# Layer 1 of a two-layer attention kernel: the head mixing as sixteen 32x32 products, transposed back on VectorE

## The chip, the cores and the metric

The kernel runs on one core of a Trainium2 chip. The metric is the device time of one execution, in microseconds, and everything is float32. The core's engines are named as in the profile: PE (TensorE, the matmuls), PEld (its weight loads), DVE (VectorE), ACT (ScalarE), POOL (GpSimd), SP (SyncE, which issues most of the DMAs). PE writes to PSUM only; DVE and ACT carry results from there to SBUF.

## The reference: what is computed

Eight images of 512 channels and 1024 tokens pass through two attention layers, each with a residual. The change is in the second one; a group norm stands before it:

```python
q, k, v = (einsum('oc,bct->bot', w, xf).reshape(b, heads, hd, t) for w in (w_q, w_k, w_v))
attn = einsum('bhdq,bhdT->bhqT', q, k) * scale
attn = einsum('gh,bhqT->bgqT', w_head, attn)          # heads are mixed before the softmax
attn = softmax(attn, axis=-1)
mean, var = attn.mean((-2, -1)), attn.var((-2, -1))   # one pair for each image and head
attn = (attn - mean) / sqrt(var + eps) * in_gamma + in_beta
out = einsum('bhqT,bhdT->bhqd', attn, v)
out = out.reshape(b, t, c) @ w_proj.T + b_proj        # without swapping heads and queries first
```

There are 8 heads of 64 channels. Since the heads are mixed before the softmax, all eight scores of a query and a key must meet before the exponential is taken. The variance over an image's whole attention map needs the sum of e and of e squared of each query and head, where e is the exponential.

## The kernel before, in words

Layer 0 takes all eight images first; layer 1 then takes them one after the other. The order of the instructions on PE, ACT, DVE, POOL and SP is the order in which the code issues them (`manual_schedule`); nothing reorders them later.

**One image in layer 1** is 32 steps x. Each handles 256 queries, 256 keys and half of the heads for the scores, and, four or five steps later, half of the keys of such a block for the rest (`half_step`, which issues everything; the lag is `MLAG`). A step has these parts:

- `scores` (L1656, twice a step): 64x64 products, four of them side by side in the array, give scores with queries on partitions. ACT (L1671) or, for some, DVE (L1669) copies them to the tile `raw`.
- `regroup` (L1680): a DMA takes every eighth partition of `raw`, so 16 queries with their 8 heads, and lays them out in the tile `re` as 128 partitions of (query, head). Each is held behind one particular matmul, so that they go one at a time.
- `mix` (L1704): `re` is the stationary operand, 64 rows of (8 queries, 8 heads) by 64 keys; the moving one is `wmix`, a block matrix of the head weights, 64 columns wide. Four 64x64 products run side by side. The result has keys on partitions and (head, query) along the row, as the last product needs it. ACT takes the exponential (L1710).
- `squares` (L1721): ACT squares e. `sum_e` (L1728) and `sum_e2` (L1732): DVE adds e and its square into running tiles.
- `values` (L1750): v is stationary, e moves with 256 columns; two column halves side by side. Four accumulators in two PSUM tiles stay open for eight steps, and `leave` copies them out (L1770, L1772).
- `totals` and `reciprocals`: for each quarter of the queries ones-products add the running sums over the partitions (L1781), and a few small operations with DMAs through DRAM make the reciprocals, which `divide` (L1840) applies.

PSUM has three tiles of two banks that scores, mixing and all projections take in turn (`m_psum`), and two banks for the accumulators. In SBUF the tile `raw` has two buffers, `re` two halves and e two buffers.

**Around the attention** stand the projections, products of 512 columns on the full array: the next image's k (started in the last steps), v (in four pieces), the output (`out1`), the next image's q (`q_projection`, whose result is written with a stride, L1512). An `Agenda` runs such work at given steps.

Of the kernel before, what the change touches and what calls it, by code (L numbers as in the profile page):

```python
# [467 lines left out]
def tile_two_attention_layers(  # L468
# [30 lines left out]
    Q8 = D // H  # L499
# [43 lines left out]

    wmix = const_tile("wmix", [P, H, Q8])
    m2 = const_tile("m2", [P, 2, Q8])
    nc.vector.reduce_sum(m2, ident.rearrange("p (a i h) -> p a i h", a=2, h=H), axis=AX.X)
    mask8 = const_tile("mask8", [P, Q8])
    nc.vector.tensor_add(mask8, m2[:, 0], m2[:, 1])
    nc.vector.tensor_scalar_mul(mask8, mask8, S1)
# [3 lines left out]
    with tc.tile_pool(name="ps_w", bufs=1, space=PSUM) as ps_w:  # L553
# [5 lines left out]
        whr.unsqueeze(2).to_broadcast([P, H, Q8]),  # L559
        mask8.unsqueeze(1).to_broadcast([P, H, Q8]),  # L560
    )

    blk8 = const_tile("blk8", [P, H])
    blk = const_tile("blk", [P, 2, H])
    nc.vector.reduce_sum(blk, ident.rearrange("p (j g i) -> p j g i", j=2, g=H), axis=AX.X)
    nc.vector.tensor_add(blk8, blk[:, 0], blk[:, 1])
# [4 lines left out]
    NQB = 4  # L571
    NCHK = B * (H + NQB)
# [91 lines left out]
    def group_stages(b0, b1, psum):  # L664
# [18 lines left out]
        return gs.means, gs.squares, end  # L683

# [12 lines left out]
    with ExitStack() as l0:  # L697
# [307 lines left out]
        def first_q1():  # L1005

            t = q_t["1"] = shared.tile([P, NT, NCC, P], F32, tag="q", name="q1_0")

            def view(a):
                return a.rearrange("p (r i j) -> p j i r", r=NR, i=Q8)  # L1010

            def finish(i, j, x, y):
                for m in range(2):
                    dst = t[:, :, 2 * i + m, ts(j, D)].rearrange("p j (i r) -> p j i r", r=NR)
                    if y is None:
                        nc.scalar.copy(dst, view(x[m]))
                    else:
                        nc.vector.tensor_add(dst, view(bank(x, m)), view(y[:, m]))

            project0("pq1_0", "q1", n_t["1"], finish)  # L1020
# [7 lines left out]
        def first_v1(i):  # L1028
# [4 lines left out]
            for m in range(2):  # L1033
                for c in range(NCC):
                    nc.tensor.matmul(
                        ps[:, m], n_t["1"][:, c, ts(2 * i + m, P)], left_t["v1"][:, c],
# [228 lines left out]
    with ExitStack() as l1:  # L1265
# [4 lines left out]
        e2pool = l1.enter_context(tc.tile_pool(name="e2pool", bufs=3))  # L1270
        zpool = l1.enter_context(tc.tile_pool(name="zpool1", bufs=1))
        upool = l1.enter_context(tc.tile_pool(name="upool", bufs=1))
        stat = l1.enter_context(tc.tile_pool(name="stat1", bufs=2))
        ps_a = l1.enter_context(tc.tile_pool(name="ps1_a", bufs=1, space=PSUM))
        ps_m = l1.enter_context(tc.tile_pool(name="ps1_m", bufs=3, space=PSUM))

        QB = T // NQB
        KB = 2 * P
        NKB = T // KB
        NX = 2 * NQB * NKB  # L1280
        QLAG = NX // NQB
        R_ORDER = (0, 4, 1, 5, 2, 6, 3, 7)
        MLAG = 4
# [10 lines left out]
        def behind(dma, ins):  # L1294

            tc.add_manual_dep(
                dma.ins,
                ins.ins.name,
                mybir.DependencyInfo(
                    mybir.DependencyClass.Sync, mybir.DependencyReason.DATA  # L1300
                ),
                reason="one at a time",
            )

        re_t = repool.tile([P, 2, H * 2 * KB], F32, tag="re", name="re")
# [57 lines left out]
        sums = [upool.tile([P, 2, FB], F32, tag=f"u{i}", name=f"sum_{i}") for i in range(2)]  # L1365
# [74 lines left out]
        def left_p(b):  # L1440

            t = rawpool.tile([P, H * 2 * KB], F32, tag="raw", name=f"left_p_{b}")
            load_left(("p", b), t[:, : 14 * HC])
# [23 lines left out]
        def v_pair(b, i):  # L1467
# [5 lines left out]
            for m in range(2):  # L1473
                for c in range(NCC):
                    nc.tensor.matmul(  # L1475
                        ps[:, m], y_t[b][:, c, ts(2 * i + m, P)], w[:, c],
# [21 lines left out]
        def q_projection(b):  # L1498
# [4 lines left out]
            def view(a):  # L1503
                return a.rearrange("p (r i j) -> p j i r", r=NR, i=Q8)

            def finish(i, j, x, y):
                for m in range(2):
                    dst = t[:, :, 2 * i + m, ts(j, D)].rearrange("p j (i r) -> p j i r", r=NR)
# [47 lines left out]
        def out1_last(a):  # L1556
# [6 lines left out]
            def products(oc, blocks):  # L1563
                if oc not in tiles:
                    tiles[oc] = m_psum(f"pp1_{b}_{oc}")
                for f in range(NFB):
                    for n in blocks:
                        nc.tensor.matmul(
                            tiles[oc][:, f], w[:, n, ts(oc, P)], out_view(b)[:, n, ts(f, FB)],
                            start=(n == 0), stop=(n == NQB - 1),  # L1570
                        )

            last = NQB - 1

            x = rawpool.tile([P, NCC, T], F32, tag="raw", name="xs_last")
            for oc in range(NCC):
                nc.sync.dma_start(out=x[:, oc], in_=x1_d[b][ts(oc, P), :])
            wsum = e2pool.tile([P, T], F32, tag="e2", name="wsum")[:, :C]
            small = ps_a.tile([P, 2, QB], F32, tag="a1", name="small_last").rearrange(
                "p m q -> p (m q)"  # L1580
            )
            off = stat.tile([P, NCC, H], F32, tag="off", name="off", bufs=1)
            for oc in range(3):
                products(oc, range(last))
                if oc == 0:
                    nc.vector.tensor_add(wsum, w[:, 0], w[:, 1])
                    for n in range(2, NQB):
                        nc.vector.tensor_add(wsum, wsum, w[:, n])
                    a.reciprocals(last)
                    a.instance()  # L1590
                    a.instance_end(small)
                    a.divide(last)
                if oc == 1:
                    pc = small[:, QB : QB + NCC * H]
# [15 lines left out]
            halves = [  # L1610
                ps_a.tile([P, 2, QB], F32, tag=f"a{f}", name=f"pp1_last_{f}").rearrange(
                    "p m q -> p (m q)"
                )
                for f in range(NFB)
            ]
            h = FB // P
            for oc in range(NCC):
                if oc < last:
                    products(oc, [last])
                for f in range(NFB):  # L1620
                    if oc < last:
                        ps = tiles[oc][:, f]
                    else:
                        ps = halves[f]
                        for n in range(NQB):
                            nc.tensor.matmul(
                                ps, w[:, n, ts(oc, P)], out_view(b)[:, n, ts(f, FB)],
                                start=(n == 0), stop=(n == NQB - 1),
                            )
                    y = e2pool.tile([P, T], F32, tag="e2", name=f"y_{oc}_{f}")[:, :FB]  # L1630
# [8 lines left out]
        class Attention1:  # L1639
            def __init__(self, b):  # L1640
                self.b = b
                self.raw, self.re, self.e, self.e2 = {}, {}, {}, {}
                self.due, self.pieces = [], []

            def scores(self, x, i):

                b, t, hp = self.b, x // 2, x % 2 * 2 + i
                qb, kb = t // NKB, t % NKB
                nm = f"s1_{b}_{x}_{i}"
                ps = m_psum(nm)  # L1650
                pv = ps.rearrange("p m (j k) -> p m j k", j=2)
                for j in range(2):
                    for c in range(2):
                        for m in range(2):
                            r = slice(m * D, m * D + D)
                            last = nc.tensor.matmul(  # L1656
                                pv[c * D : c * D + D, m, j],
                                qo_t[b][r, 2 * qb + j, hp, ts(c, D)],
                                k_t[b][r, hp, ts(kb, KB)], start=True, stop=True,
                            )  # L1660
                if x > MLAG:
                    self.piece(last)
                if x % 2 and i == 1:
                    self.due = [(t, r) for r in R_ORDER]
                if x % 2 == 0 and i == 0:
                    self.raw[t] = rawpool.tile([P, H, 2, KB], F32, tag="raw", name=f"raw_{b}_{t}")
                dst = self.raw[t][:, 2 * hp : 2 * hp + 2]
                if i == (x == 0) and (x < MLAG or x % 2):
                    nc.vector.tensor_copy(dst, pv)  # L1669
                else:  # L1670
                    nc.scalar.copy(dst, pv)  # L1671

            def regroup(self, ins=None, n=1):


                for t, r in self.due[:n]:
                    self.re[t, r] = re_t[:, (t + self.b) % 2].rearrange(
                        "p (r j k) -> p r j k", r=NR, k=KB
                    )[:, r]
                    dma = nc.sync.dma_start(out=self.re[t, r], in_=self.raw[t][r::NR])  # L1680
                    if ins is not None:
                        behind(dma, ins)
                self.due = self.due[n:]

            def piece(self, ins=None, n=1):
# [376 lines left out]
```

## Time and profile before

| | |
|---|---|
| time, three runs | 4219.67 us median (4215.69 to 4220.82) |
| span of the profiled execution, first to last instruction | 4215.8 us |
| granted PE clock, mean | 0.999 |
| PE busy in the span | 4147.3 us (98%) |
| DVE busy | 2868.0 us (68%) |
| ACT busy | 2318.4 us (55%) |
| POOL busy | 60.3 us (1%) |
| mean DMA rate | 126 GB/s |
| layer 1, first and last score product | 1800.5 and 4147.9 us |

The span equals the fastest of the three runs to 0.1 us, so what lies around it is below what the runs differ by. Layer 1 begins at about 1800 us and takes some 302 us for an image. A float32 product is recorded as two MATMULs with a weight load each, so the counts of the PE rows are twice those in the code. Busy time is the union of overlapping instructions: of products that run side by side only the joint time counts, and the mean duration of one contains the way through the array.

### The profile page before, as it was taken

To read this page: it belongs to the slowest core of one execution; us is meant where nothing else is said; L and a number is where in the kernel's file an instruction comes from. 1 tells how busy PE (TensorE), PEld (TensorE's weight loads), DVE (VectorE), ACT (ScalarE), POOL (GpSimd) and SP (SyncE) were. 2 spreads that over 40 slices of the span, in tenths; PEclk is the share of its full clock that TensorE was granted. 3 is DMA by queue.
4 is the path that set the end of the run, shared out by engine and by line. 5 is a ranking of instruction groups with operands and counts; after the bars stand their busy time and mean duration, and the time that the engine had idled before them with its cause. 6 is when DMAs were issued, how large, how long until landed. Compare 5 with 4: busy or idle time off the path is not lost.

```text
span 4215.8 us, 131422 instructions
## 1 busy us (share of the span) xinstructions
PE 4147.3 (98%) x58572; PEld 2216.2 (53%) x58572; DVE 2868.0 (68%) x3779; ACT 2318.4 (55%) x2735; POOL 60.3 (1%) x86
## 2 busy tenths in 40 slices
PE   8999999999999999999999999999999999999998
PEld 4353535353535353466466466466466466465565
DVE  5748484848484747568668668578578588587587
ACT  2717171727272625258268278278287287286386
POOL 0000000000000000000000000000000000000000
PEclk9999999999999999999999999999999999999999
DMA  4212121212121212167467377377386386485575
GB/s 132 97 65 94 59 101 50 82 45 84 48 84 48 84 48 84 62 156 196 131 170 188 121 189 189 108 201 190 104 206 177 112 208 159 129 209 145 148 180 138
DMA packets 257905, 529.35 MB, mean 126 GB/s; under 512 B 52336, under 2 KB 59888, under 8 KB 250672
## 3 DMA queue, kind: packets, MB, share of 16 engines
q1 hardware_dynamic: 254752, 520.15, 43.5%
q8 instruction: 461, 7.55, 0.8%
q0 software_dynamic: 2576, 0.69, 0.4%
q14 instruction: 116, 0.95, 0.1%
HBM read 204.50 MB, written 46.92 MB: 60 GB/s over the span
## 4 chain that ended last, share of the span: by engine, by line
PE 93%; DMA 2%; DVE 2%; ACT 1%; issue 1%; SPq 0%; DVEq 0%; ACTq 0%
PE a L1750 12%; PE m L1704 12%; PE s L1656 11%; PE s L1082 10%; PE a L1108 10%; PE pk_p L902 5%; PE pq_p L902 5%; PE pv_p L902 5%; PE pp_p L902 5%; PE pk L1400 4%; PE pq L1400 4%; PE pv L1475 4%; PE pp L1400 3%; PE t L1781 1%; DMA re<-raw 1%
## 5 line engine op out<-in xcount | busy, mean ns | idle before, releaser
L1704 PEld LDWEIGHTS m<-wmix,re 64*64 64x64 f32 x32768 | 583.6, 135 | 119.6 <-issue 53.5
L1087 ACT ACTIVATE e<-s 128x1024 f32<-128x1024 f32 x512 | 497.2, 1026 | 234.3 <-PE s L1082 233.8
L1704 PE MATMUL m<-wmix,re 64*64 64x64 f32 x32768 | 596.5, 219 | 21.1 <-issue 14.0
L1710 ACT ACTIVATE e<-m 128x1024 f32<-128x1024 f32 x512 | 525.2, 1026 | 141.9 <-PE m L1704 137.2
L1728 DVE TENSOR_TENSOR z<-z,e 128x1024 f32<-128x1024 f32 x448 | 538.0, 1219 | 68.8 <-ACT e L1710 68.7
L1732 DVE TENSOR_TENSOR z<-z,e 128x1024 f32<-128x1024 f32 x448 | 535.1, 1220 | 66.3 <-ACT e L1721 64.7
L1750 PE MATMUL a<-e,v 128*64 128x256 f32 x4096 | 556.2, 392 | 1.7 <-issue 1.0
L1656 PE MATMUL s<-k,q 64*64 64x256 f32 x8192 | 552.0, 388 | 5.0 <-DVE q L1512 2.7
L1095 DVE TENSOR_TENSOR zacc<-zacc,e 128x1024 f32<-128x1024 f32 x384 | 468.7, 1221 | 79.1 <-ACT e L1087 56.8
L1671 ACT COPY raw<-s 128x1024 f32<-128x1024 f32 x368 | 372.6, 1013 | 265.5 <-PE s L1656 226.5
L1082 PE MATMUL s<-q,k 64*64 64x512 f32 x4096 | 490.1, 593 | 2.3 <-ACT e L1087 2.3
L1108 PE MATMUL a<-e,v 64*64 64x512 f32 x4096 | 484.0, 589 | 0.0
L1721 ACT ACTIVATE e<-e 128x1024 f32<-128x1024 f32 x448 | 459.8, 1056 | 0.0
L1656 PEld LDWEIGHTS s<-k,q 64*64 64x64 f32 x8192 | 268.5, 132 | 267.8 <-issue 164.4
L1750 PEld LDWEIGHTS a<-e,v 128*64 128x64 f32 x4096 | 250.8, 136 | 122.5 <-issue 14.0
L1108 PEld LDWEIGHTS a<-e,v 64*64 64x64 f32 x4096 | 156.7, 133 | 282.8 <-issue 282.5
L1082 PEld LDWEIGHTS s<-q,k 64*64 64x64 f32 x4096 | 147.9, 133 | 275.2 <-issue 241.0
L1669 DVE COPY raw<-s 128x1024 f32<-128x1024 f32 x144 | 175.9, 1222 | 93.5 <-PE s L1656 89.7
L1093 DVE TENSOR_TENSOR zacc<-e,e 128x1024 f32<-128x1024 f32 x64 | 78.3, 1223 | 53.6 <-ACT e L1087 53.6
L1475 PE MATMUL pv<-wv,y 128*128 128x512 f32 x256 | 114.1, 599 | 0.5 <-DVE raw L1669 0.5
L1480 DVE COPY v<-pv 128x512 f32<-128x512 f32 x30 | 20.7, 690 | 136.0 <-ACT v L1479 136.0
L902 PE MATMUL pv_p<-left_v,tmp 128*128 128x256 f32 x512 | 113.1, 379 | 0.0
(316 smaller groups left out, 4162.7 us busy)
## 6 DMA issues: line engine op xcount, KB each, us to landing
re<-raw SPq DMA_DIRECT2D x1024, 256.0 KB
rzb<-zd SPq DMA_DIRECT2D x256, 128.0 KB
left_q<-left_q SPq DMA_DIRECT2D x17, 1792.0 KB
left_p<-left_p SPq DMA_DIRECT2D x17, 1792.0 KB
left_k<-left_k SPq DMA_DIRECT2D x10, 1792.0 KB
x<-in_x_dram SPq DMA_DIRECT2D x32, 512.0 KB
x<-x SPq DMA_DIRECT2D x64, 256.0 KB
left_v<-left_v SPq DMA_DIRECT2D x8, 1792.0 KB
```

The lines of the kernel that those rows point to most:

```text
L902: nc.tensor.matmul(out, st, mv, start=start, stop=(k == 1), skip_group_check=True)
L1082: nc.tensor.matmul(ps[c * D : c * D + D, m], k[r, hp, k0 : k0 + D], q[r, hp, ts(f, FB)], start=True, stop=True,)
L1087: nc.scalar.activation(e[i], ps, AF.Exp, scale=S0 * S0)
L1095: nc.vector.tensor_add(zacc[g], zacc[g], e[i])
L1108: nc.tensor.matmul(acc[g][a][m * D : m * D + D], v[rows, kc, ts(2 * hp + m, D)], e[i][rows, m], start=(kc == 0), stop=(kc == NG - 1),)
L1400: nc.tensor.matmul(self.ps[m][:, i], w[:, left, k * HC + i * P : k * HC + i * P + P], right[:, k], start=(k == 0 and m != 2), stop=(k == 1 ...
L1656: last = nc.tensor.matmul(pv[c * D : c * D + D, m, j], qo_t[b][r, 2 * qb + j, hp, ts(c, D)], k_t[b][r, hp, ts(kb, KB)], start=True, stop=True,
L1704: last = nc.tensor.matmul(ps[c * D : c * D + D, a, ts(r, D)], self.re[t, r][rows, j, k0 : k0 + D], wmix[rows].rearrange("p g i -> p (g i)" ...
L1710: nc.scalar.activation(self.e[y][:, j], ps.rearrange("p a c -> p (a c)"), AF.Exp)
L1728: nc.vector.tensor_add(self.z[:, j], self.z[:, j], self.e[y][:, j])
L1732: nc.vector.tensor_add(self.z2[:, j], self.z2[:, j], self.e2[j])
L1750: last = nc.tensor.matmul(self.acc[w][two * D : two * D + D, s].rearrange("p (c i) -> p c i", i=Q8), v_t[b][:, kc, ts(g, D)], e[:, g], sta ...
```

## The change

Layer 1 now has eight passes p of 128 queries for an image, each in four steps t, and what the engines do in them is another:

- **Mixing.** `wmix` shrinks to 32 columns (8 heads by 4 queries) and becomes the stationary operand; `re` moves, 512 columns at a time. Sixteen 32x32 products stand side by side: four row groups by four column groups. The result has (head, query) on partitions and keys along the row. Each mixing takes two of the three PSUM tiles.
- **Transposition.** After the exponential, `flip` turns e by 32x32 blocks on DVE, one instruction of 128x2048 elements a step, into the tile `et`, which has keys on partitions again. It reads 32 elements eight apart for each column of a block; the token order of v (`tokens`) is changed to suit.
- **Sums.** `moments` runs batch-norm statistics over e, four instructions of 512 elements a step. They give mean and squared deviation of the even and of the odd elements; the access pattern alternates between two halves of the tile that lie 4 KiB apart, so that each is one query. `totals` makes the sums from them. The squares on ACT, both running sums on DVE and the ones-products over 1024 columns go.
- **Values.** v is stationary as before, `et` moves with 64 columns.
- **Scores** have 512 columns in place of 256, and ACT copies all of them but four of the first pass.
- **DMAs.** `regroup` is issued at fixed places of the steps: three (query half, slot) pairs in steps 1 and 2, five at the end of step 3, two DMAs each. `re` has one buffer of four slots. The reciprocals' DMAs are on POOL's queue, for the last pass on SP's.

```diff
-    Q8 = D // H
+    QX = P // NR
...
+    def tokens(y, c, kb):
+        return y[:, c].rearrange("p (r kb) -> p kb r", kb=NT)[:, kb]
...
             def scores(self, p, i):
+                b, kh, hp = self.b, i // 4, i % 4
+                ps = m_psum(f"s1_{b}_{p}_{i}")
+                for c in range(2):
+                    for m in range(2):
+                        r = slice(m * D, m * D + D)
+                        nc.tensor.matmul(
+                            ps[c * D : c * D + D, m], qo_t[b][r, p, hp, ts(c, D)],
+                            k_t[b][r, hp, ts(kh, FB)], start=True, stop=True,
+                        )
...
+            def regroup(self, kh, s):
+                for r in range(2):
+                    nc.sync.dma_start(
+                        out=re_t[:, s, r, ts(kh, FB)], in_=self.raw[kh][2 * s + r :: NR]
+                    )
...
+            def mix(self, p, s):
+                b = self.b
+                ps = [m_psum(f"m1_{b}_{p}_{s}_{h}") for h in range(2)]
+                for c in range(4):
+                    for a in range(4):
+                        rows = slice(a * 32, a * 32 + 32)
+                        nc.tensor.matmul(
+                            ps[a // 2][c * 32 : c * 32 + 32, a % 2].rearrange("p (r k) -> p r k", r=2),
+                            wmix[rows].rearrange("p g i -> p (g i)"),
+                            re_t[rows, s, :, ts(c, 2 * P)],
+                            start=True, stop=True, tile_position=(a * 32, c * 32),
+                        )
+                e = self.e[p, s] = epool.tile([P, 2, 4, 2 * P], F32, tag="e", name=f"e1_{b}_{p}_{s}")
+                for h in range(2):
+                    nc.scalar.activation(
+                        e[:, :, 2 * h : 2 * h + 2].rearrange("p r a k -> p a r k"),
+                        ps[h].rearrange("p a (r k) -> p a r k", r=2), AF.Exp,
+                    )
+
+            def flip(self, p, s):
+                u, st = s // 2, s % 2
...
+                dst = self.et[p, u].rearrange("p kb g (st x q) -> p st x kb g q", st=2, q=4)[:, st]
+                nc.vector.transpose(dst, self.e[p, s].rearrange("p r a (k kb) -> p (r a) kb k", kb=8))
+
+            def moments(self, p, s):
...
+                for a in range(4):
+                    nc.vector.bn_stats(
+                        self.bn[p][:, s, a], e[:, :, a].rearrange("p r k -> p k r")
+                    )
+
+            def values(self, p, u, half):
...
+                for kb in range(4 * half, 4 * half + 4):
+                    for s in range(4):
+                        for two in range(2):
+                            g = 2 * s + two
+                            nc.tensor.matmul(
+                                acc[two * D : two * D + D, s], v_t[b][:, kb, ts(g, D)], et[:, kb, g],
+                                start=(kb == 0 and s == 0), stop=(kb == 7), skip_group_check=True,
+                            )
...
+            def step(self, p, t, ag):
+                first = p < NT
+                if first and t < 3:
+                    self.scores(p, 2 * t)
+                    self.scores(p, 2 * t + 1)
+                if t == 0 and p >= 2:
+                    self.values(p - 2, 1, 0)
+                if p >= 1:
+                    self.mix(p - 1, t)
+                    self.flip(p - 1, t)
+                    if t == 3:
+                        self.moments(p - 1, 2)
+                    if t != 2:
+                        self.moments(p - 1, t)
+                k_leave()
+                if first and t == 3:
+                    self.scores(p, 6)
+                    self.scores(p, 7)
+                ag.run(4 * p + t - 0.5)
+                if t == 1 and p >= 2:
+                    self.totals(p - 2)
+                    self.values(p - 2, 1, 1)
+                    self.leave(p - 2, 1)
+                if t >= 2 and p >= 1:
+                    self.values(p - 1, 0, t - 2)
+                    if t == 3:
+                        self.leave(p - 1, 0)
+                if first:
+                    for kh, s in {1: ((0, 0), (0, 1)), 2: ((0, 2),)}.get(t, ()):
+                        self.regroup(kh, s)
+                    if t == 3:
+                        self.regroup(0, 3)
+                        for s in range(4):
+                            self.regroup(1, s)
+                if p >= 1:
+                    self.piece(2)
+                if t == 0 and p >= 4 and p % 2 == 0:
+                    self.divide(p // 2 - 2)
+                ag.run(4 * p + t)
...
-            def half_step(self, x, ag):
-                y, w = x - MLAG, x - MLAG - 1
-                if 0 <= w < NX:
-                    self.squares(w, 0)
-                    self.sum_e(w, 0)
-                if x < NX:
-                    self.scores(x, 0)
...
```

In `values` the tiles `et` and `acc` are those of the pass and half; `leave` copies each accumulator out with two ACT copies of 64x256 elements. The projections stay as they are, but four of k's seven products are issued in the last pass, where all seven were issued in the last steps before.

## The prediction

> **What bounds the kernel now.** I read the page's totals and chain first, then layer 1 by stretches, one step in order of time, and the groups by shape.
>
> ```profile
> PE 4147.3 (98%) x58572; PEld 2216.2 (53%) x58572; DVE 2868.0 (68%) x3779; ACT 2318.4 (55%) x2735; POOL 60.3 (1%) x86
> ...
> PE 93%; DMA 2%; DVE 2%; ACT 1%; issue 1%; SPq 0%; DVEq 0%; ACTq 0%
> ```
>
> PE never rests, and 93% of the chain that ended last is PE's. By stretch (an image of layer 1, then one of its 32 steps; columns: length, then busy time of PE, PEld, DVE, ACT, POOL):
>
> ```profile
> 2406.00:2708.00 302.00, 299.18 (x5923) 181.39 (x5922) 219.89 (x255) 186.07 (x209) 6.77 (x9) 1.00 0.62 165
> ...
> 2500.88:2506.82 5.94, 5.94 (x181) 4.24 (x177) 4.25 (x5) 5.08 (x6) 1.67 (x2) 1.00 0.60 132
> ```
>
> An image takes 302 us, a step 5.94: 32 steps are 190 us and 112 are the rest (v, k, output and q projections, fill and drain). Four steps do the work of one pass of the changed kernel, so the number to beat is 23.76 us a pass. DVE has 82 us free in 302, no more; that matters below.
>
> The prices, from groups by shape (busy us together, mean ns of one; PE records are two to a product):
>
> ```profile
> L1704 PE MATMUL m<-wmix,re 64*64 64x64 f32 x32768 | 596.5, 219 | 21.1 <-issue 14.0 <-DMA re<-raw 5.7
> L1656 PE MATMUL s<-k,q 64*64 64x256 f32 x8192 | 552.0, 388 | 5.0 <-DVE q L1512 2.7 <-DVE v L1040 1.4 <-ACT raw L1671 0.9
> L1082 PE MATMUL s<-q,k 64*64 64x512 f32 x4096 | 490.1, 593 | 2.3 <-ACT e L1087 2.3
> L1781 PE MATMUL t<-z,ones 128*32 128x512 f32 x512 | 62.6, 598 | 0.9 <-DVE z L1732 0.9
> L1710 ACT ACTIVATE e<-m 128x1024 f32<-128x1024 f32 x512 | 525.2, 1026 | 141.9 <-PE m L1704 137.2
> L1671 ACT COPY raw<-s 128x1024 f32<-128x1024 f32 x368 | 372.6, 1013 | 265.5 <-PE s L1656 226.5 <-DMA re<-raw 21.9 <-DMA left_k<-left_k 4.8
> ...
> L1164 DVE TENSOR_TENSOR xa<-xa,u 128x512 f32<-128x512 f32 x64 | 44.3, 692 | 2.2
> L1512 DVE TENSOR_TENSOR q<-pq,sum 128x512 f32<-128x512 f32 x42 | 43.2, 1070 | 11.5 <-PE pq L1400 11.5
> L648 DVE BATCH_NORM_STATS2 bn_o<-x 128x6 f32<-128x512 f32 x64 | 40.8, 681 | 0.0
> ```
>
> See three things. Products of small tiles overlap: a mixing record costs 18.2 ns (596.5/32768) though one lasts 219. Four column tiles at once run at full rate (L1781: 62.6/512 x 4 = 489 ns for four records of 512 columns). And L1512 costs 1070 ns where the same 512 elements read in a row cost 692 (L1164): its sources hop 256 bytes at every element, and that costs (1070 - 692)/512 = 0.74 ns an element. (Not because one source is in PSUM: v<-pv_p,tmp, L978, also lasts 692.)
>
> **What the Trainium skill says.** "Vector Engine (DVE) Microarchitecture Reference", 5.2 Measured stream behaviour on trn2: a port keeps full rate only if consecutive elements come as pairs of adjacent words; hopping at every element costs 1.73 ns a column in place of 1.05 for large hops and 2.50 for a small step (24 words); one stream that alternated between two regions kept the full rate. L1512 agrees: (1070 - 692)/512 + 1.04 = 1.78. The same page, 3.8 The reshape front-end, says that the block transposition sustains one element per cycle and lane; no run here shows it. "TensorE: Matmul & The Clock Gate", Part 3, gives 10.6-fold for sixteen 32x32 tiles at 512 columns; the trace shows only four tiles at once[...].
>
> **The change, part by part, for one pass.** Layer 0 stays as it is.
>
> PE. Scores: 32 products, 64 records at 490.1/4096 = 119.7 ns: 7.7 us (before 4 x 16 x 2 records at 67.4: 8.6). Mixing: sixteen tiles; two records of 489 ns each plus the start of twelve more tiles, about 0.1: 1.06 x 4 = 4.2 (before 512 x 18.2 ns = 9.3). Values: 128 products of 64 columns, 256 records, two side by side; a 64-column record with its weight load held its tile 4 x 18.2 = 73 ns in the mixing, so 128 x 73 = 9.3 (before 64 x 135.8 ns = 8.7). The ones-products shrink to nothing. Sum 21.2, at most 2.5 below the old pass. v's projection loads weights with a step of eight elements; its loads of 0.19 stand under products of 0.44 and would stay there at twice that. Should the load of 64 columns (some 55 ns, what L1656 loses: 4 x 67.4 - 213) not hide under so short a product, values are 128 x 110 = 14 and the pass 26.
>
> ACT. Eight copies at 1.013, eight exponentials at 1.026, four copies out at 0.365 (L1772): 17.8. The squares (8 x 1.056 a pass) are gone. Hidden under PE's 21.2; alone it would be the bound at 17.8.
>
> DVE. Removed: 14 additions of 1.22 a pass, most of the score copies and half of the copies out. Added: 4 transpositions of 2048 elements, 16 statistics of 512, totals, half a division. Durations overlap a little when instructions follow each other unheld; in order of time two additions of 1.22 take 2.35, 0.08 less:
>
> ```profile
> 2340.43 2.35 DVE L1732 TENSOR_TENSOR z<-z,e 128x1024 f32<-128x1024 f32 x2
> ```
>
> So 1024 elements take 1.13 and 512 take 0.60: 1.04 ns an element and 0.07 us.
> - Statistics: 0.68 - 0.08 = 0.60, x16 = 9.6. They alternate between two regions; the page's case kept full rate, so I take 0.60. If L1512's 0.74 ns applies, +0.38 each, +6.1.
> - Transposition: contiguous 2.20. It reads elements 32 bytes apart, never a pair. With L1512's price +1.52: 3.72. With the page's small-step price 2.50 x 2048 = 5.2. I take 3.72, the measured hop: 14.9 a pass; ends 8.8 and 20.7.
> - Totals: about eleven operations at 0.2 (128x8 rows last 0.17): 2.2; division 1.22/2 = 0.6.
> Sum 27.3, ends 21.2 and 33.1 (39 if the statistics pay too). This is over PE's 21.2, so DVE becomes the bound and what PE saves is lost.
>
> What waits for it: an e tile stays taken until its statistics end; there are two. A late DVE holds back the exponential; that stands in ACT's order before the next score copies, so PSUM stays full (mixing alone takes two of three tiles) and PE stops. Nothing decouples them.
>
> DMAs. As many regroup DMAs as before, 128 of 256 KB an image, but ten of a pass's sixteen come at its end, in SP's order, at 0.53 us of issue each; pieces queue behind them. The next pass's first mixing needs the third and fourth of the ten, which wait for the last two score copies (2 x 1.01, behind two exponentials of 1.03): 4.1 us, four issues of 0.53, then the transfers, for which no median is shown (an 8 KB transfer on POOL's queue takes 3.8 from issue to landing), so about 9 us. Cover on PE is two score pairs at 1.9 and two value halves at 2.3, 8.4 us. With DVE as the bound, PE arrives later and the DMAs are hidden; with a free DVE they could cost 1 us a pass or more. POOL's reciprocals are used two passes later, and only its own next DMA stands behind them.
>
> Outside the passes: 107 us, worked as follows. Before the first transposition 28 (eight scores 7.7, two v pieces of 7.1, two scores, mixing, exponential); 7 of DVE work for the next k in the last pass; after it 72 (k remainder, v and the rest of the sums 16; output 24.6, that is 56 records of 512 columns at 112.5/256 = 0.44 by pq_p in L902; v 7; q 24.6). I take 110, as the old kernel's own remainder is 112.
>
> Sum: 8 x 27.3 x 1.01 + 110 = 331 us an image, +29; eight images +232. From the span: 4216 + 232 = 4448 us. The span equals the fastest run and is 0.1% under the median, so I forecast 4450.
>
> **The rivals.**
> - A, faster: transpositions read at one element a cycle whatever the step (3.8 of the page taken alone). DVE 21.2, PE 21.2, coupled 22 a pass: 286 an image, -16 x 8 = -128: 4090. It decides at a pass of (302 - 110)/8 = 24.0 us, so at a transposition below (24.0/1.01 - 9.6 - 2.8)/4 = 2.8 us. Against it: L1512. For it: L1512 is another operation with two sources, one of them in PSUM.
> - B, small step dear: 5.2 us each, 33.4 a pass: 377, +75 x 8 = +600: 4820. The same time if the transposition pays 0.74 and the statistics too.
> - C, both dear: 39.2 a pass, 427: 5200.
> - D, the mixing does not overlap sixteen-fold or the short values do not hide their loads: PE 26 or more. With dear transpositions DVE covers it; with cheap ones it gives 8 x 27 + 110, about 4430.
> - E, DVE cheap but the burst of DMAs late by 1 to 3 us at each pass: 4150 to 4280.
>
> **How the numbers follow.** Forecast 0.33 (own range 4380 to 4540), A 0.19, B 0.29, C 0.07, D 0.07, E 0.05. The range 4080 to 4850 holds the forecast, D, E, half of A and most of B: about 0.8. 0.2% (8 us) is about what a measurement can tell from no change. Faster: A and part of E, 0.20; same 0.02; slower 0.78.
>
> **What would show it.** STREAM_TRANSPOSE rows by mean: near 3.8 us the forecast, 2.3 A, 5.2 B. Statistics at 0.68 or 1.06. In passes DVE should be busy 98% and PE about 75%, the chain mostly DVE, and ACT waiting. Sixteen mixing products should take 1.1 us, a value half 2.3. I am wrong if DVE idles inside passes, or if PE still leads the chain.

## The result: slower by 18%, and the profile after

| | before | after |
|---|---|---|
| time, median of four runs | 4219.34 us (4215.69 to 4220.82) | 4972.73 us (4970.45 to 4976.36) |
| ratio, 95% interval | | 1.179 (1.178 to 1.181) |
| span of the profiled execution | 4215.8 us | 4968.7 us |
| granted PE clock, mean | 0.999 | 0.917 |

The direction was forecast, the size was not: 4450 was predicted, and 4972.73 lies outside the range of 4080 to 4850. The page of the changed kernel, its totals, the granted clock in 40 slices (layer 1 begins in slice 15), and four groups (busy us together, mean ns of one, idle time of the engine before them and who ended it):

```profile
PE 4132.0 (83%) x41932; PEld 2029.9 (41%) x41932; DVE 3289.7 (66%) x4340; ACT 1962.9 (40%) x2431; POOL 71.0 (1%) x126
...
PEclk9999999999999998898898889889889889889887
...
L1692 DVE STREAM_TRANSPOSE et<-e 128x2048 f32<-128x2048 f32 x256 | 995.2, 3901 | 558.7 <-ACT e L1679 558.7
...
L1700 DVE BATCH_NORM_STATS2 bn<-e 128x6 f32<-128x512 f32 x1024 | 629.4, 690 | 0.0
...
L1744 PE MATMUL z<-sel,zz 128*32 128x32 f32 x256 | 38.8, 245 | 647.9 <-DVE zz L1739 643.7
...
L1669 PE MATMUL m<-re,wmix 32*32 32x512 f32 x8192 | 409.8, 625 | 1.3 <-ACT raw L1647 1.0
```

The two new operations on DVE cost what was forecast: a transposition 3.90 us (3.80 forecast), statistics 0.69 (0.68). But no engine is full. DVE is idle 558.7 us ahead of transpositions, waiting for the exponential, and PE is idle 647.9 us ahead of a product that itself takes 38.8 us in all: z, which `totals` issues once in a pass (64 waits, 10 us each).

Stretches of the third image of layer 1, its first pass and its fifth (columns: length, then busy time of PE, PEld, DVE, ACT, POOL; then the clock, the DMA share and GB/s). `totals` runs two passes after the one it sums, so the first pass has none; it also lacks one of the four halves of the values products, 2.1 us on PE:

```profile
2639.14:2666.60 27.46, 23.23 (x388) 10.88 (x384) 25.12 (x20) 15.85 (x19) 0.00 (x0) 0.88 0.66 155
2778.20:2814.00 35.80, 23.85 (x456) 12.93 (x452) 26.82 (x31) 16.68 (x22) 1.15 (x2) 0.86 0.53 122
```

The first pass takes 27.46 us, and 27.6 was forecast for all of them (with 2.2 of totals in it). From the second on they take 37.2 (mean over seven images, from first transposition to first transposition), with little more work on any engine. The fifth pass in order of time (start, length, engine; in brackets the idle time before and its releaser):

```profile
2778.26 3.90 DVE L1692 STREAM_TRANSPOSE et<-e 128x2048 f32<-128x2048 f32 x1 [0.56 <-ACT e L1679]
...
2782.08 2.46 DVE L1700 BATCH_NORM_STATS2 bn<-e 128x6 f32<-128x512 f32 x4
2784.45 3.84 DVE L1692 STREAM_TRANSPOSE et<-e 128x2048 f32<-128x2048 f32 x1
2788.20 2.47 DVE L1700 BATCH_NORM_STATS2 bn<-e 128x6 f32<-128x512 f32 x4
2790.57 0.17 DVE L1739 TENSOR_SCALAR zz<-bn 128x16 f32<-128x16 f32 x1
...
2791.41 0.66 PE L1744 MATMUL z<-sel,zz 128*32 128x32 f32 x4 [10.97 <-DVE zz L1739]
...
2792.00 3.40 PE L1716 MATMUL a<-et,v 128*64 128x64 f32 x64
...
2795.34 1.95 PE L1635 MATMUL s<-k,q 64*64 64x512 f32 x16
...
2797.22 1.65 PE L1669 MATMUL m<-re,wmix 32*32 32x512 f32 x32
2798.79 2.08 PE L1716 MATMUL a<-et,v 128*64 128x64 f32 x64
2798.97 1.94 ACT L1679 ACTIVATE e<-m 128x1024 f32<-128x1024 f32 x2 [0.51 <-ACT raw L1647]
...
2800.94 3.93 DVE L1692 STREAM_TRANSPOSE et<-e 128x2048 f32<-128x2048 f32 x1 [7.85 <-ACT e L1679]
```

This is a loop through two in-order queues. In step 1, z stands on PE ahead of the values, the next scores and the next mixing. It needs zz, six operations of 0.2 us, and they stand on DVE behind two transpositions and eight statistics: from 2778.26 to 2791.4, 13.1 us. PE waits 10.97 of them. Then it is DVE's turn: its next transposition needs the exponential of the mixing that PE could not start, so 7.85 us are lost there. The two engines work in turns where they should work side by side. (The chain that ended last covers only 9% of the span in this trace and cannot show this; the groups and the order of time do.)

### The profile page after: what moved, and what is told of

Read it like the earlier page. It is cut to its first block, busy times and chain, and to the rows that moved or that the text cites. A ratio compares the mean times of both kernels' runs of the same rounds, so it can differ in the third digit from the quotient of the medians.

```text
span 4968.7 us, 96367 instructions
## 1 busy us (share of the span) xinstructions
PE 4132.0 (83%) x41932; PEld 2029.9 (41%) x41932; DVE 3289.7 (66%) x4340; ACT 1962.9 (40%) x2431; POOL 71.0 (1%) x126
## 5 line engine op out<-in xcount | busy, mean ns | idle before, releaser
L1692 DVE STREAM_TRANSPOSE et<-e 128x2048 f32<-128x2048 f32 x256 | 995.2, 3901 | 558.7 <-ACT e L1679 558.7
L1716 PE MATMUL a<-et,v 128*64 128x64 f32 x16384 | 648.7, 249 | 79.6 <-DVE et L1692 79.6
L1716 PEld LDWEIGHTS a<-et,v 128*64 128x64 f32 x16384 | 610.5, 163 | 237.3 <-DVE et L1692 129.9
L1700 DVE BATCH_NORM_STATS2 bn<-e 128x6 f32<-128x512 f32 x1024 | 629.4, 690 | 0.0
L1744 PE MATMUL z<-sel,zz 128*32 128x32 f32 x256 | 38.8, 245 | 647.9 <-DVE zz L1739 643.7
L1635 PE MATMUL s<-k,q 64*64 64x512 f32 x4096 | 541.9, 626 | 26.8 <-ACT e L1679 19.9
L1647 ACT COPY raw<-s 128x1024 f32<-128x1024 f32 x480 | 465.5, 1024 | 174.5 <-PE s L1635 140.6
L1669 PE MATMUL m<-re,wmix 32*32 32x512 f32 x8192 | 409.8, 625 | 1.3 <-ACT raw L1647 1.0
L1635 PEld LDWEIGHTS s<-k,q 64*64 64x64 f32 x4096 | 125.4, 137 | 359.3 <-issue 179.9
L1462 PE MATMUL pv<-wv,y 128*128 128x512 f32 x480 | 215.1, 603 | 0.3 <-ACT raw L1647 0.3
L1669 PEld LDWEIGHTS m<-re,wmix 32*32 32x32 f32 x8192 | 103.3, 105 | 179.0 <-ACT raw L1647 61.9
L1462 PEld LDWEIGHTS pv<-wv,y 128*128 128x128 f32 x480 | 148.9, 315 | 63.4 <-issue 5.7
L1387 PE MATMUL pk<-right,left_k 128*128 128x512 f32 x224 | 107.1, 621 | 17.4 <-ACT e L1679 17.4
```

Of the source, the lines that this page charges most:

```text
L1462: nc.tensor.matmul(ps[:, m], tokens(y_t[b], c, 2 * i + m), w[:, c], start=(c == 0), stop=(c == NCC - 1),)
L1635: nc.tensor.matmul(ps[c * D : c * D + D, m], qo_t[b][r, p, hp, ts(c, D)], k_t[b][r, hp, ts(kh, FB)], start=True, stop=True,)
L1647: nc.scalar.copy(dst, ps)
L1669: nc.tensor.matmul(ps[a // 2][c * 32 : c * 32 + 32, a % 2].rearrange("p (r k) -> p r k", r=2), wmix[rows].rearrange("p g i -> p (g i)"), r ...
L1692: nc.vector.transpose(dst, self.e[p, s].rearrange("p r a (k kb) -> p (r a) kb k", kb=8))
L1700: nc.vector.bn_stats(self.bn[p][:, s, a], e[:, :, a].rearrange("p r k -> p k r"))
```

## The experiments

Theory L is this loop. Against it stand D (DVE's own work sets the pass, and its idle time only mirrors it), C (the lower granted clock of PE sets it), and S (it is the late reciprocals, which keep one of three PSUM tiles taken, and not zz). The letters are those of the expectations below; the prediction's rivals C and D are others. In all experiments with an edit to `totals`, the six operations on zz are a method of their own, `parts`; `totals` keeps the z product and the reciprocals. What was measured of all kernels (pass: mean of the second to seventh interval between first transpositions, seven images; image: the same from image to image):

| kernel | median us | ratio to before (95%) | pass | image | clock |
|---|---|---|---|---|---|
| changed kernel | 4972.73 | 1.179 (1.178 to 1.181) | 37.2 | 399.5 | 0.917 |
| d1: zz ahead of four statistics | 4831.85 | 1.147 (1.145 to 1.149) | 34.9 | 382.1 | 0.932 |
| e1: zz at the start of the pass | 4492.35 | 1.066 (1.064 to 1.068) | 27.7 | 340.0 | 0.972 |
| e2: z and reciprocals ahead too | 4526.02 | 1.074 (1.072 to 1.077) | 27.7 | 345.0 | 0.967 |
| e3: contiguous transposition | 4698.18 | 1.115 (1.113 to 1.117) | 33.7 | 365.1 | 0.940 |
| e4: e2 and e3 | 4312.45 | 1.023 (1.021 to 1.025) | 25.2 | 320.0 | 0.980 |
| z1: e4, PSUM tile free earlier | 4273.99 | 1.014 (1.012 to 1.016) | 24.8 | 314.2 | 0.984 |
| b1: z1, values between | 4256.26 | 1.011 (1.009 to 1.012) | 24.9 | 311.3 | 0.989 |
| b2: b1, statistics in step | 4251.04 | 1.009 (1.007 to 1.011) | 25.0 | 311.2 | 0.987 |
| b3: b2, loads spread | 4220.28 | 1.001 (1.000 to 1.002) | 24.5 | 307.3 | 0.990 |
| b4: b3, last pass | 4164.61 | 0.987 (0.985 to 0.989) | 24.3 | 299.4 | 0.993 |

The old kernel was timed again beside each group of kernels (the changed kernel; e1 to e4; d1 and z1 to b2; b3 and b4), with medians of 4213.7 to 4219.3 us. A difference between kernels of two groups is therefore good to some 6 us.

**e1: zz first.**

```diff
+                if t == 0 and p >= 2:
+                    self.parts(p - 2)
                 if p >= 1:
                     self.mix(p - 1, t)
                     self.flip(p - 1, t)
...
                 if t == 1 and p >= 2:
                     self.totals(p - 2)
```

> Edit: the six small VectorE operations of totals (zz) are issued at the start of step t=0, ahead of flip and moments; the z product and the reciprocals stay where they were. Theory L (a loop through the in-order queues: PE stands 10 us a pass at the z product because zz stands behind two transpositions and eight statistics on DVE): PE no longer waits for zz. But the z result holds one of the three PSUM tiles until the reciprocals, which still stand behind flip and moments of step 1, so the mixing of step 2 comes late by 2 to 3 us: a pass of 30 to 31 us against 37, time 4600 to 4700. Rival D (DVE's own work sets the pass, and its idle time only mirrors it): 4950 to 4980, no change. Rival C (PE's lower granted clock sets it): no change beyond 1%.

4492.35 us, below L's range: six operations of 0.2 us, moved by one step, are worth 480 us. The wait of z is almost gone, and the rest of L's expectation was too cautious: the reciprocals do hold PE (42.7 us in all, shown below), but in the passes DVE sets the pace all the same. Two groups of the kernel, and six of its passes (together 165.50 us; busy PE, PEld, DVE, ACT, POOL):

```profile
L1692 DVE STREAM_TRANSPOSE et<-e 128x2048 f32<-128x2048 f32 x256 | 999.1, 3912 | 99.8 <-ACT e L1679 99.6
...
L1749 PE MATMUL z<-sel,zz 128*32 128x32 f32 x256 | 22.4, 207 | 29.6 <-DVE zz L1739 28.6 <-DVE zz L1741 0.2
```

```profile
sum 165.50, PE 142.57 PEld 74.43 DVE 164.09 ACT 100.40 POOL 6.90; mean PE 23.76 PEld 12.41 DVE 27.35 ACT 16.73 POOL 1.15
```

DVE is busy 164.09 of 165.50 us, 99%, with 27.35 us a pass. Theory D is out for the changed kernel: the same DVE work took 37.2 us there. It holds for this one, which is the kernel that the prediction described. Theory C is out as a cause: the clock rises from 0.917 to 0.972 by moving six VectorE operations, so it follows the waits.

**e2: the z product and the reciprocals too.**

```diff
+                if t == 1 and p >= 2:
+                    self.totals(p - 2)
                 if p >= 1:
                     self.mix(p - 1, t)
...
-                    self.totals(p - 2)
                     self.values(p - 2, 1, 1)
```

> Edit: as the first one, and the z product with its reciprocals is issued before the mixing of step t=1 instead of after its statistics, so nothing of totals stands behind a transposition of the same step. Theory L: the passes take what the first pass of each image, which has no totals, takes already (27.5 us), plus 1 to 2 us for the totals themselves: 4430 to 4520, DVE over 92% busy in passes. Rival D: 4950 to 4980. Rival C: within 1% of the changed kernel, with the clock still 0.92.

4526.02, just above L's range, and 34 us slower than e1, although more was taken out of the way. The passes are the same, 27.7: DVE sets them. The loss is in the last pass of an image, from its first to its last transposition 34.9 us against 30.5. The z product now comes ahead of the mixing, and its PSUM tile is asked for again by the second half of that mixing, before the reciprocals are through. From the waits (engine, line, releaser; us in all, times, longest), first e1, then e2:

```profile
PE m L1669 <- DVE r L1779: 42.7, 29, 4.6
```

```profile
PE s L1635 <- DVE r L1779: 101.9, 40, 3.3
PE m L1669 <- DVE r L1779: 57.7, 7, 8.3
```

**d1: a dose.** Only zz moves, and only by four statistics.

```diff
                     self.flip(p - 1, t)
+                    if t == 1 and p >= 2:
+                        self.parts(p - 2)
...
                         self.moments(p - 1, t)
```

> Edit: of the changed kernel, only the six small VectorE operations of totals move, and only ahead of the four statistics of the same step (they stay behind both transpositions). A dose test of theory L: what stands ahead of zz on VectorE gets shorter by 4 x 0.62 = 2.5 us, so the wait of the z product falls by 2.5 us each, and seven passes of an image get 2.5 us shorter: 4972 - 56 x 2.5 = 4830 (4800 to 4850). Rival S (not the zz but the late reciprocals, which hold the z result's PSUM tile, block PE; these stay where they are): 4960 to 4985.

4831.85 us, 141 less (135 when each is set against the old kernel timed beside it), where L asked for 140 and S for nothing. So it is the time that zz stands behind, one for one: 141/56 = 2.5 us for four statistics of 0.62. The waits of the changed kernel and of this one:

```profile
PE z L1744 <- DVE zz L1739: 643.7, 64, 13.9
```

```profile
PE z L1749 <- DVE zz L1739: 509.4, 64, 11.5
```

**e3: the stride of the transposition.** For contiguous reads the keys are dealt out differently: the mixing's moving operand takes them in runs of 32.

```diff
-        return y[:, c].rearrange("p (r kb) -> p kb r", kb=NT)[:, kb]
+        return y[:, c, ts(kb, P)]
...
-                            re_t[rows, s, :, ts(c, 2 * P)],
+                            re_t[rows, s].rearrange("p r (kb c k) -> p c r kb k", c=4, k=32)[:, c],
...
-                nc.vector.transpose(dst, self.e[p, s].rearrange("p r a (k kb) -> p (r a) kb k", kb=8))
+                nc.vector.transpose(dst, self.e[p, s].rearrange("p r a (kb k) -> p (r a) kb k", k=32))
```

> Edit: the transposition reads its 32 elements next to each other. To suit, the mixing's column group c takes keys kb*128 + c*32 + k (moving reads in runs of 32), and v's token blocks are contiguous. Order of the work as in the changed kernel. If the step of eight is what makes it 3.9 us, the transposition falls to 2.2 or 2.3 us and v's weight loads from 315 back to 190 ns. Theory L: of a 37 us pass about 20 us are DVE's stretch before zz (two transpositions in it) and 17 the way around through PE and ACT back to DVE, with two more: a pass gets 4 to 6.5 us shorter, time 4560 to 4720, and DVE's idle time before the transposition stays above 400 us. If the transposition's time comes from its writes (runs of four words) or its operation: 3.9 us as before and 4960 to 4985.

4698.18, as L has it. One transposition falls from 3.90 to 2.31 us, which saves 404 us of DVE work (995.2 to 590.9), and the time falls by 275. The first pass takes 22.2 us, the others 33.7, and DVE is idle longer than before, since the way around through PE and ACT has not become shorter:

```profile
L1692 DVE STREAM_TRANSPOSE et<-e 128x2048 f32<-128x2048 f32 x256 | 590.9, 2308 | 703.6 <-ACT e L1679 702.8
...
L1744 PE MATMUL z<-sel,zz 128*32 128x32 f32 x256 | 37.4, 238 | 456.1 <-DVE zz L1739 451.3 <-DVE zz L1741 1.1
```

**e4: both.** The edits of e2 and e3 together.

> Edit: both, the contiguous reads of the transposition and all of totals ahead. Theory L: DVE needs 4 x 2.2 + 16 x 0.62 + 3 = 21.7 us a pass and PE 22 to 23, so a pass of 23 to 24.5: time 4160 to 4300, about the old kernel's. If a burst of DMAs at the end of the pass then comes late, up to 2 us more a pass: 4430. Rival D, with a transposition of 2.2 us: 4972 less 64 x 6.8 = 4540.

4312.45, a little above L's range, and still 2.3% over the old kernel. Against e2 DVE has 404 us less to do, and 214 of them came. The passes are 25.2 us with PE at 22 and DVE at 20.6 of them, so nothing is the bound; PE loses its 3 us in short waits. The longest wait of a mixing is in the last pass of an image, in order of time:

```profile
3289.78 1.05 PE L1669 MATMUL m<-re,wmix 32*32 32x512 f32 x4
3290.31 2.46 DVE L1700 BATCH_NORM_STATS2 bn<-e 128x6 f32<-128x512 f32 x4
...
3292.69 1.21 DVE L1802 TENSOR_TENSOR q<-q,rzb 128x1024 f32<-128x1024 f32 x1
3293.82 1.22 DVE L1362 TENSOR_TENSOR right<-y 128x1024 f32<-128x1024 f32 x1
3295.07 1.22 DVE L1362 TENSOR_TENSOR right<-y,right 128x1024 f32<-128x1024 f32 x1
3296.21 0.34 DVE L1760 RECIPROCAL rz<-z 32x32 f32<-32x32 f32 x1
...
3297.02 2.01 PE L1669 MATMUL m<-re,wmix 32*32 32x512 f32 x28 [6.19 <-DVE r L1779]
```

The mixing has begun and stops after four of its 32 records: its second PSUM tile is the one of z, and the reciprocals that free it stand behind four statistics, the division and two additions for the next k. This is the loop again, with another link.

**z1 to b4: one wait after another.** z1 puts the statistics of step 0 behind the reciprocals. b1 puts each half of the values products one step later and ahead of the mixing. b2 puts the statistics of step 2 back into their step.

```diff
                 if t == 1 and p >= 2:
                     self.totals(p - 2)
+                if t == 1 and p >= 1:
+                    self.moments(p - 1, 0)
+                if t < 3 and p >= 2:
+                    self.values(p - 2, *((0, 1), (1, 0), (1, 1))[t])
                 if p >= 1:
                     self.mix(p - 1, t)
...
+                if t == 3 and p >= 1:
+                    self.values(p - 1, 0, 0)
```

> Edit: of the kernel with contiguous transposition and totals ahead (4312), the statistics of step 0 move behind the reciprocals, so that the z result's PSUM tile is free 2.5 us earlier. The trace of that kernel shows PE held by that tile 0.4 to 0.6 us in a pass and 6.2 us in the last pass of an image: 7 x 0.5 + 6.2 = 9.7 us an image, 78 in all: 4235 (4215 to 4270). If other tiles hold PE at the same places anyway: 4290 to 4315.

> Edit: the one before, and each half of the values products is issued one step later and ahead of the mixing of its step, so that PE has 2.1 us of work between the score products and the next mixing, while ACT empties the PSUM tiles. In the kernel with 4312 PE loses about 3.4 us in each pass in short waits for PSUM tiles. Half of that gone: 7 x 1.7 = 12 us an image off the one before: 4140 (4110 to 4190). If the DMAs of the next pass (0.25 to 1.9 us late at the first mixing there) become the bound instead: no gain on the one before, 4215 to 4260.

> Edit: the one before, with the statistics of step 2 ahead of the transposition of step 3 instead of behind it. The e tile of step 2 comes free 2.3 us earlier, the transposition of step 3 comes 2.5 us later. Values no longer need it early: within 15 us of the one before, 10 us faster if the exponential of the next pass waits for that tile. If the values products wait for the last transposition: up to 8 x 2 us slower.

z1 brought 38 us of 78 (34 when each is set against the old kernel timed beside it): the longest wait of the mixing for the reciprocals fell from 6.2 to 3.8 us only, because the division and the two additions still stand ahead of them. b1 brought 18 of 95 and lies in the range of its second case: most of PE's waits were passed on. The waits of the score copies on ACT for the DMAs that empty `raw`, in z1 and then in b1:

```profile
ACT raw L1647 <- DMA re<-raw: 55.6, 24, 5.8
```

```profile
ACT raw L1647 <- DMA re<-raw: 117.6, 37, 6.5
```

b2 brought 5. b3 then spreads the loads for the next image, which SP issues among the regroups, and b4 moves the copies out of the accumulators behind the next score copies, the division by one step, and the first k product of the next image ahead of the last pass's mixing, with its additions half a step later.

```diff
-                    self.piece(2)
+                    self.piece(2 if t == 0 else 1)
...
-                if t == 0 and p >= 4 and p % 2 == 0:
-                    self.divide(p // 2 - 2)
+                if t == 3 and p >= 3 and p % 2:
+                    self.divide((p - 3) // 2)
...
-                ag.at(4 * NT - 0.5, lambda: right_tile(b + 1))
-                ag.at(4 * NT - 0.5, lambda: k_go(1))
-                ag.at(4 * NT, lambda: right_y(b + 1, [0, 1]))
+                ag.at(4 * NT - 1, lambda: right_tile(b + 1))
+                ag.at(4 * NT - 1, lambda: k_go(1))
+                ag.at(4 * NT + 0.5, lambda: right_y(b + 1, [0, 1]))
```

> Edit: of the kernel with 4251, the loads of the next image's y and of k's weights (30 DMAs an image) are issued five in a pass instead of eight. The passes 1 to 3 of the first seven images take 26.5, 24.8 and 26.2 us there, at a DMA share of 0.85 to 0.95, and 23.6, 24.1 and 23.7 in the last image, which has only small loads. If the loads crowd the regroup DMAs: 5 us an image for seven images, 35 in all: 4216 (4205 to 4235). If it is only that the SP queue issues them ahead of the regroups: the same sign, 10 to 20 us. If neither: within 8 us.

> Edit: the one before, and four moves by a fraction of a pass: the copies out of the values' accumulators stand behind the next score copies on ACT, the division goes one step earlier, and in the last pass the first product of the next k comes ahead of the mixing and its VectorE additions one half step later. PE waits there 2.9 us for a regroup DMA and 1.25 us for the reciprocals in the last pass of an image, 1 us in three passes for the division, and 0.36 us in a pass for a score copy behind a copy out: 9 us an image at most, 72 in all; I expect two thirds: 4170 (4140 to 4205), below the old kernel's 4214. If the waits only move to the next one in line: 4205 to 4230.

b3 brought 31 us of 35, and the score copies' waits for the regroup DMAs fell from 116.8 us in b2 to 87.9, so the loads did hold up the regroups; whether by crowding the DMA engines or by standing ahead in SP's order, only the size speaks (35 was expected of the first, 10 to 20 of the second). b4 brought 56, where two thirds of 72, so 48, were expected. In b4 the last pass takes 21.4 us from first to last transposition, against 27.9. It is 1.3% faster than the old kernel, with the same sixteen-tile mixing, block transposition and statistics as the changed one. PE is busy 95% of the span again:

```profile
PE 3964.2 (95%) x41932; PEld 1821.0 (44%) x41932; DVE 2884.4 (69%) x4340; ACT 1949.7 (47%) x2431; POOL 71.0 (2%) x126
```

## Why the prediction was wrong

**The step that failed** is the sentence "This is over PE's 21.2, so DVE becomes the bound", with its sum of 27.3 us taken as the pass. A sum of one engine's work is the pass only if that engine never waits. The prediction costed `totals` as work: "about eleven operations at 0.2" on DVE, and on PE "the ones-products shrink to nothing". The work is that small. For waits inside a pass the prediction allowed a factor of 1.01, 0.3 us, and gave no reason for it; the changed kernel's pass is 37.2 us for 27.35 of DVE work. The z product has a place in PE's order and zz one in DVE's, but nothing in the prediction asked what stands behind z on PE and ahead of zz on DVE. e1 takes only this away and lands at 4492; d1 gives the slope. So 480 of the 523 us between forecast and result are this loop, and 42 are the rest.

**"Nothing decouples them"** was written of the e tiles and PSUM, and of a late DVE that holds up PE. It was half the mechanism: a late PE holds up DVE in the same way, and with both halves the engines take turns.

**The prices** were right. The transposition: 3.90 us against 3.80, and with the stride gone 2.31 against 2.28 (the pitch of 2.20 and 0.08), so a hop of 32 bytes costs (3.90 - 2.31)/2048 = 0.78 ns an element, where L1512 gave 0.74 (by its code L1512 reads both sources with a stride and writes in runs of 64 elements). The Trainium skill, "Vector Engine (DVE) Microarchitecture Reference", 5.2 Measured stream behaviour on trn2, has 1.73 ns a column for one source that hops 4 KiB at every element, and 2.50 where both sources, or the destination, step by 24 words; the prediction took the second for a single source. The measured 3.90/2048 = 1.90 is nearer to the first, although the step is small. The prediction's rivals B and C are out with that. The statistics, alternating between two regions, kept their rate: four of them take 2.46 us, 0.615 each (0.60 forecast). DVE's pass was forecast at 27.3 us and is 27.35 in e1.

**PE:** a half of the values takes 2.08 us (2.3 forecast), two score products 1.95 (1.9), a mixing of sixteen products 1.14 to 1.22 where nothing holds it (1.06), and a pass of e4 has 22.0 us of PE work (21.2). The weight loads of a half of the values take 1.95 us beside its 2.08. The prediction's rival D is out; its own sum, 8 x 27 + 110 = 326 us an image, gives 4408 and not 4430. The 213 ns in the price of a weight load stand in no trace: records of 256 columns took 113.1/512 = 0.221 us before (pv_p, L902), which leaves 49 ns for the load, not 55.

**Outside the passes** an image takes 340.0 - 8 x 27.7 = 118 us in e1. The forecast's 302 and 112 are means over all eight images, of which the last is shorter (295.6 us in e1, not 340.0), so the mean of e1 has to be set against its 331: from 1800.0 us, the first score product, to the end at 4487.7 it is 336.0, with 114 outside the passes, where 110 was forecast. Eight times 5 us is 40 of the 42 that are the rest of the miss.

**Rival A** said that the change wins if the transposition is below 2.8 us. In e3 and e4 it is 2.31, and they take 4698 and 4312, not 4090. That rival had the same fault as the forecast: it took the larger of the engines' sums, with 0.8 us for their coupling, for the pass: 22 us. e4 has 25.2, and b4, the last of the repaired kernels, 24.3. **Rival E**, DMAs late by 1 to 3 us at each pass, is what appears once DVE is free: in e4 mixings wait for them 41 times, 48.3 us in all and 4.4 at the longest, and the score copies wait for them too (117.6 us in b1).

**What would show it:** of the signs that the prediction named, "I am wrong if DVE idles inside passes" is the one that came: DVE is 75% busy (26.82 of 35.80) and PE 67%, not 98% and 75%. In e1, where the loop is gone, DVE has its 99%, and PE 86% (23.76 us a pass, some of it at half clock).

## What to carry to other kernels

An instruction that is cheap on two engines can cost more than the dear ones: for each product, note what stands behind it in its own queue and what stands ahead of its operand in the other, and add up the way around before you take one engine's sum for the time. The first pass of a pipeline, which has no work of earlier passes in it, is a free experiment: where it is much faster than the next and has nearly the same work, look for an order and not for a price. When a stall is taken out, the next one in line takes part of the gain (38 us of 78, 18 of 95), so repairs of a few per cent have to be measured one by one.

## What the runs showed of the hardware

- PE's clock fell to half around waits, and not always during them. Stretches of the changed kernel's pass shown above, from the wait of 10.97 us on (the seventh number from the left is the mean clock, after the length and five busy times):

```profile
2780.00:2791.40 11.40, 0.45 (x17) 0.02 (x1) 11.30 (x15) 1.99 (x3) 0.00 (x0) 0.71 0.46 103
2791.40:2793.00 1.60, 1.53 (x22) 1.34 (x24) 1.09 (x7) 0.00 (x0) 0.25 (x1) 0.50 0.00 0
2793.00:2795.40 2.40, 2.40 (x56) 2.33 (x54) 0.09 (x1) 0.00 (x0) 0.35 (x1) 0.59 0.06 9
2795.40:2797.20 1.80, 1.80 (x18) 0.45 (x16) 0.00 (x0) 1.39 (x3) 0.55 (x1) 1.00 0.00 0
```

Here the clock fell during the wait and came back some 3.5 us after PE had started again. In e1, PE stood from 2636.32 to 2638.23:

```profile
2636.00:2638.20 2.20, 0.32 (x14) 0.00 (x0) 2.20 (x2) 1.77 (x2) 0.00 (x0) 1.00 0.33 78
2638.20:2641.50 3.30, 3.27 (x72) 3.15 (x76) 3.23 (x10) 0.16 (x1) 0.41 (x1) 0.58 0.51 112
2641.50:2643.00 1.50, 1.50 (x38) 0.46 (x40) 1.50 (x1) 0.00 (x0) 0.19 (x1) 0.78 0.07 3
```

There the clock was full through the wait of 1.92 us and fell only after PE had started again, for some 3.4 us ((0.42 x 3.30 + 0.22 x 1.50)/0.5, if it is either full or half). A half of the values takes 3.40 us in the first case and 2.08 at full clock, so the loop pays 1.3 us a pass for it, on the way around. The Trainium skill, "TensorE: Matmul & The Clock Gate", Part 1, HAM oscillation, speaks of gaps longer than about 3.4 us. The first case agrees; in e1 a fall followed a wait of 1.92 us, and none followed one of 3.02 us (from 2712.3 us, clock 1.00 up to 2722). What decides there was not tried.
- A weight load of 128x128 takes 315 ns when it reads with a step of eight elements and 190 when contiguous (L1462, the changed kernel and e4). It is hidden under the products: a record takes 215.1/480 = 0.448 us there and 212.1/480 = 0.442 here.
- A moving operand read in runs of 32 elements (e4) was no slower: a mixing that nothing holds takes 1.14 us there and 1.22 in the changed kernel.
